# Two row groups for B.C, and a new order of the work around it, in a two-directional state-space kernel

## The chip, the cores and the metric

The kernel runs on one core of one Trainium2 chip. A core has five engines that run side by side and meet at semaphores: TensorE (PE in the profile; its weight loads, which overlap its matmuls, are PEld), VectorE (DVE), ScalarE (ACT), GpSimd (POOL) and SyncE (SP), which issues most of the DMAs. Matmuls write to PSUM[...]; everything else lies in SBUF. The metric is the time of one execution in device microseconds.

## The reference

The input x is 8 sequences of 512 tokens with 256 features. Each goes through a layer norm, a state-space layer in both directions and a linear layer with a low-rank correction:

```python
def _mamba2(x, Win, convw, convb, dtb, Alog, Dsk, normw, Wout):
    z, xBC, dt = split(x @ Win)                  # 512, 512 + 64 + 64, 8
    xBC = _silu(causal_conv4(xBC, convw) + convb)
    xs, Bm, Cm = split(xBC)                      # xs: 8 heads of 64
    dt = softplus(dt + dtb)
    dA = exp(dt * -exp(Alog))
    h_t = dA_t * h_{t-1} + outer(dt_t * xs_t, B_t)
    y_t = C_t . h_t + Dsk * xs_t
    y = y * _silu(z)
    y = y * rsqrt(mean(y * y) + 1e-05) * normw
    return y @ Wout

x = x + concat([fwd(ln(x)), flip(bwd(flip(ln(x))))]) @ Wo + bo
x = x + (ln(x) @ W.T + b + (ln(x) @ V_r) @ C.T)
```

Everything is computed in float32.

## The kernel before

A sequence is cut into four chunks of 128 tokens (NC = 4). Inside a chunk the recurrence becomes matrix work: B.C of all pairs of tokens of the chunk (a 128x128 matrix per direction, `cb`), times the decays between the two tokens, which a scan on VectorE makes (`scan`), gives the matrix `lam` (`mix` multiplies the two); `lam` times the scaled inputs `xdt` gives the chunk's own part of y, and the state at the chunk's edge times `dec` (decays times C) gives the rest. A **pair** is chunk c of the forward direction with chunk 3 - c of the backward one; there are 32, and the main loop (line 817) takes one per pass, i = 0 to 31. Pass i finishes pair p = i (`outputs`, `evict`, `times_gate`, `square`) and prepares pair q = i + 1 (`turn`, `cb`, `gate`, `scale_x`, `scan`, `skip`, `mix`, `scale_c`). Between them stand up to four blocks of a later sequence's projection and convolution (`work[0]` to `work[3]`: `project` on TensorE, `tap` on ScalarE, `convolve` on VectorE, `silu` on ScalarE) and the tail of an earlier chunk (`t`: output projection `project`, `residual`; `t0`, one pass later: `scales`, `norm2`, `bias2`, `turn`, `ffn`, `add_ffn`). Every eight passes (two sequences) a group of short VectorE steps for softplus and the decays is added (`st`).

The order of the instructions on each engine is that of the program text: `pin` ties each instruction to the one before it on its engine. So moving a call moves it in every queue that it issues to.

**PSUM.** The banks are given out by four pools: `p_seed` 1, `p_proj` 3 (`pp` of a projection, `pz` of the gate, `pst` of the state), `p_tr` 2 (`pxs`, `pxt`, `pxh` and other transposes, `ss`, `ptot`, `pcb`) and `p_y` 2 (`py` of both directions, then `pf` and `pm` of the tail; `pwy` and `pwf` in the first passes). A tile waits for the bank's last reader.

**cb before.** For one pair, B of both directions stands in 128 partitions (`bb`: 64 state rows of the forward direction, then 64 of the backward one). C stands twice: in `cc`, laid out like `bb`, for `scale_c`, and in `cbd`, block-diagonal, 128 columns per direction with zeros elsewhere. One matmul of 128 rows and 256 columns gives both directions' B.C. `silu` of the block that holds B and C writes all three copies (line 421), each of 64 partitions x 512. Memsets at line 171 zero `cbd`.

Names that the change and the steps touch, with their lines: `Block.silu` L415/L423, `Pair.turn` L496/L498, `scale_x` L507, `cb` L514, `mix` L520, `skip` L528, `gate` L538, `gate_silu` L545, `decay_state` L553, `outputs` L563, `add_state` L583 to L589, `evict` L593, `times_gate` L597, `square` L600, `norm_sum` L605, `norm_mean` L609, `norm_power` L612, `presum` L618; `Tail.bias1` L633, `project` L640, `residual` L647, `norm2` L657, `bias2` L668, `turn` L673/L675, `ffn` L680, `add_ffn` L683; `prepare_wf` L212/L213; `scale_c` L479; `steps_last` L345, `steps_total` L361; `turn1` L257/L258; `tokenwise_b` L432/L434.

Of the kernel before, what the change touches and what calls it, by code (L numbers as in the profile page):

```python
# [8 lines left out]
F32 = mybir.dt.float32  # L9
AF = mybir.ActivationFunctionType  # L10
ALU = mybir.AluOpType
# [3 lines left out]
P = 128  # L15
NB, L, DM = 8, 512, 256
NC = L // P
DI = 512
NS = 64
# [12 lines left out]
def tile_bimamba_ffn(  # L32
# [55 lines left out]
    def ps(p, shape, name):  # L88
        return p.tile(shape, F32, name=name, tag=p.name)
# [76 lines left out]
    pool.tensor_tensor(fold, ident[:, :64], ident[:, 64:], ALU.add)  # L166

    cbd = []
    for i in range(2):
        cbd.append(const.tile([P, NC, 2, P], F32, name=f"cbd{i}"))  # L170
        pool.memset(cbd[i], 0.0)

# [193 lines left out]
    class Block:  # L366
# [45 lines left out]
        def silu(self):  # L412
# [7 lines left out]
            bs, cs = slice(0, NS), slice(NS, P)  # L420
            for to, rows in ((s["bb"], bs), (cbd[b % 2][:, :, d, :], cs), (s["cc"], cs)):
                half = to[d * NS:(d + 1) * NS]
                act.activation(  # L423
                    half if d == 0 else half[:, ::-1, :],
                    self.acc[rows, :].rearrange("p (c t) -> p c t", c=NC), AF.Silu,
                )
# [12 lines left out]
    class Pair:  # L439
# [71 lines left out]
        def cb(m):  # L511

            m.pcb = ps(p_tr, [P, 2, P], f"cb_{m.name}")
            pe.matmul(  # L514
                m.pcb.rearrange("p d t -> p (d t)"), lhsT=m.s["bb"][:, m.c, :],
                rhs=cbd[m.b % 2][:, m.c].rearrange("p d t -> p (d t)"), start=True, stop=True,
            )

        def mix(m, d):
            dve.tensor_tensor(  # L520
                m.lam[d], m.lam[d], m.pcb[:, d, :].unsqueeze(1).to_broadcast([P, NH, P]), ALU.mult
            )
# [54 lines left out]
        def add_state(m):  # L577
            if m.c == NC - 1:
                return
            pst = ps(p_proj, [P, DI], f"pst_{m.name}")  # L580
            for d in range(2):
                rows = slice(d * NS, (d + 1) * NS)
                pe.matmul(pst[rows, :], lhsT=m.s["bn"][:, m.c, rows], rhs=m.xw[d], start=True, stop=True)  # L583
            if m.c == 0:
                m.h_new = m.tile("h", (P, DI))
                act.copy(m.h_new, pst)
            else:
                dve.tensor_tensor(m.h_new, m.h_new, pst, ALU.add)
            m.s["h"] = m.h_new  # L589
# [227 lines left out]
    for i in range(n):  # L817
# [12 lines left out]
        if (c == 0 if even else c == 1) and b + 3 < NB:  # L830
            load(b + 3)
        when(t0, "scales", "norm2", "bias2")
        p.decay_state()
# [4 lines left out]
        p.add_state()  # L838
        when(before, "norm_sum", "norm_mean")
        if q:  # L840
            for d in range(2):
                q.turn(d)
        when(work[0], "project", "tap")
        when(t0, "turn")
# [5 lines left out]
        if st and not even and c == 2:  # L850
            st.exponential()
        if q:
            q.cb()
            q.gate(0)
            q.gate_silu(0)
            for d in range(2):
                q.scale_x(d)
            q.scan(0)
        if q:
# [8 lines left out]
        if st and not even and c == 2:  # L868
# [3 lines left out]
            pairs[i + 2].fetch()  # L872
        when(t0, "ffn", "add_ffn")
        when(before, "norm_power")
        if q:
            q.scale_c()
        when(t, "bias1")
        p.presum()
# [15 lines left out]
        if i < 2:  # L894
            prepare_wy(i, range(2, NBLK))
        if q:
            q.skip(1)
        when(work[1], "convolve")
        if i == 2:
            prepare_wf()  # L900
        if i == 0:
# [10 lines left out]
        if even and c in (1, 3) and ahead < NB:  # L912
            turn1(ahead + (c == 3), 0)
            turn1(ahead + (c == 3), 1)
        if c == 2 and b + 1 < NB:
            tokenwise_b(b + 1)
# [75 lines left out]
```

## Time and profile before

| What | Value |
|---|---|
| median of 3 runs | 665.66 us (665.1 to 667.6) |
| the profiled execution | 668.52 us, its span 666.5 us |
| granted TensorE clock, mean of the span | 0.983 |
| matmul records of cb (L514) | 64, mean 397 ns, 20.1 us in all |
| SiLU into cbd (L423) | 16, median 628 ns |
| scale_c (L479) / bias1 (L633) / bias2 (L668), one | 2.36 / 0.73 / 0.73 us |
| GpSimd's bias2 waits for ScalarE's norm2 | 71.5 us in all, 29 times |
| VectorE's convolution waits for ScalarE's tap | 41.9 us in all, 24 times |
| VectorE's residual waits for GpSimd's bias1 | 16.5 us in all, 10 times |

How to read it: the profile is one execution with a hardware profiler. A row of a timeline has the start, the length, the engine, the line of the kernel, the operation, output<-inputs, the shape, and xN for N records that follow each other; in brackets stands how long the engine had been idle before, and what ended that. A float32 matmul leaves two records (four for a sum over two halves of the features); [...]the rate is read from start to start. A wait for several semaphores is put down to the last one by the profile. A row of the table of stretches has start:end and length, then for each engine its busy time and number of instructions, in the order PE, PEld, DVE, ACT, POOL, then the granted clock, the DMA share and GB/s.

### The profile page before, as it was taken

Reading aid. Unit: us, or ns where it says so; the run is one execution under the profiler, and the core shown is the slowest. Engines: PE = TensorE matmul, PEld = TensorE weight load, DVE = VectorE, ACT = ScalarE, POOL = GpSimd, SP = SyncE. Lnnn points to the kernel's source line nnn. Section 1 sums busy time; section 2 is a strip of 40 time slices with the busy share of each in tenths; the row PEclk is TensorE's granted clock in tenths of the full one; section 3 lists DMA queues with packets and bytes.
Section 4 is the critical chain, followed back from the end, with each engine's and each line's share of the span. In section 5 each row is a group of like instructions: output and inputs, shape, how many; then the busy total and the mean of one; then the engine's idle time right before and its main releaser. Section 6 shows DMA issues by size and latency. Waiting matters only on the chain.

```text
span 666.5 us, 12446 instructions
## 1 busy us (share of the span) xinstructions
PE 623.3 (94%) x4652; PEld 478.5 (72%) x4652; DVE 542.0 (81%) x827; ACT 399.8 (60%) x855; POOL 467.2 (70%) x572
## 2 busy tenths in 40 slices
PE   4968998999999999999999999999999998999996
PEld 2556676777776777877777677777877777787785
DVE  4788888788988899977988998877998887886643
ACT  2787565876566565875476574686576654564421
POOL 4447455677854888757856789638876679599983
PEclk9979998999999999999999998999999998999998
DMA  7555332313055312134045322332005432333010
GB/s 207 161 168 143 111 104 49 86 42 102 18 182 142 112 62 90 59 92 143 17 135 147 92 64 80 112 112 103 25 13 179 104 111 80 111 112 111 17 49 32
DMA packets 34940, 64.63 MB, mean 97 GB/s; under 512 B 7680, under 2 KB 22080, under 8 KB 34880
## 3 DMA queue, kind: packets, MB, share of 16 engines
q1 hardware_dynamic: 32736, 63.79, 31.8%
q8 instruction: 37, 0.61, 0.4%
q10 hardware_dynamic: 2144, 0.04, 0.2%
q14 instruction: 23, 0.19, 0.1%
HBM read 59.10 MB, written 4.72 MB: 96 GB/s over the span
## 4 chain that ended last, share of the span: by engine, by line
PE 51%; DVE 24%; POOL 13%; ACT 7%; issue 4%; DVEq 0%; POOLq 0%; ACTq 0%
PE pm L640 11%; PE pp L379 9%; PE pz L538 9%; PE py L563 9%; DVE xc L397 7%; DVE lam L490 4%; PE pf L680 3%; POOL yg L597 3%; DVE lam L520 3%; PE pxs L496 3%; POOL xdt L507 2%; PE pdt L275 2%; DVE x L647 2%; ACT xc L390 2%; PE pst L583 2%
## 5 line engine op out<-in xcount | busy, mean ns | idle before, releaser
L397 DVE SCALAR_TENSOR_TENSOR xc<-pp,conv_sb,xc 128x511 f32<-128x511 f32 x183 | 136.0, 744 | 46.3 <-ACT xc L390 41.9
L379 PE MATMUL pp<-xhT,win_sb 128*128 128x512 f32 x320 | 151.2, 600 | 0.5 <-ACT xhT L710 0.5
L490 DVE TENSOR_TENSOR_SCAN lam<-lam,seed 128x512 f32<-128x512 f32 x128 | 145.6, 1200 | 0.0
L538 PEld LDWEIGHTS pz<-xhT,win_sb 128*128 128x128 f32 x1024 | 125.7, 194 | 10.3 <-issue 7.7
L538 PE MATMUL pz<-xhT,win_sb 128*128 128x128 f32 x1024 | 126.6, 277 | 0.0
L640 PE MATMUL pm<-wy,yg 128*128 128x256 f32 x512 | 115.5, 379 | 0.0
L640 PEld LDWEIGHTS pm<-wy,yg 128*128 128x128 f32 x512 | 97.1, 190 | 13.1
L379 PEld LDWEIGHTS pp<-xhT,win_sb 128*128 128x128 f32 x320 | 57.8, 194 | 45.7 <-issue 42.6
L528 ACT ACTIVATE yg<-xc,dcol 128x128 f32<-128x128 f32 x256 | 80.9, 393 | 0.0
L390 ACT ACTIVATE xc<-pp,conv_sb 128x512 f32<-128x512 f32 x64 | 49.3, 774 | 44.9 <-PE pp L379 44.7
L520 DVE TENSOR_TENSOR lam<-lam,cb 128x1024 f32<-128x1024 f32 x64 | 75.0, 1212 | 0.1
L668 POOL TENSOR_TENSOR x<-x,bf_sb 128x256 f32<-128x256 f32 x32 | 23.3, 729 | 73.6 <-ACT xh L657 71.5
L507 POOL TENSOR_TENSOR xdt<-xs,dw 128x512 f32<-128x512 f32 x64 | 66.5, 1046 | 6.6 <-ACT xs L498 6.6
L563 PE MATMUL py<-lam,xdt 128*64 128x128 f32 x1024 | 66.3, 285 | 0.0
L415 ACT ACTIVATE xc<-xc 128x512 f32<-128x512 f32 x64 | 39.5, 628 | 43.7 <-DVE xc L397 43.4
L563 PEld LDWEIGHTS py<-lam,xdt 128*64 128x64 f32 x1024 | 58.6, 143 | 7.5 <-issue 4.6
L593 DVE TENSOR_TENSOR yg<-py,yg 128x512 f32<-128x512 f32 x64 | 42.2, 685 | 18.0 <-PE py L563 15.5
L507 POOL TENSOR_TENSOR xs<-xs,dw 128x512 f32<-128x512 f32 x48 | 50.1, 1045 | 3.8
L647 DVE SCALAR_TENSOR_TENSOR x<-pm,rms,x 128x256 f32<-128x256 f32 x64 | 30.9, 483 | 25.4 <-POOL x L633 16.5
L496 PE MATMUL pxs<-ident,xc 128*128 128x128 f32 x256 | 39.7, 286 | 12.5 <-ACT rms L609 5.1
L498 ACT COPY xs<-pxs 128x512 f32<-128x512 f32 x64 | 36.1, 586 | 15.4 <-PE pxs L496 15.2
L496 PEld LDWEIGHTS pxs<-ident,xc 128*128 128x128 f32 x256 | 29.8, 151 | 19.2 <-ACT rms L609 6.8
(445 smaller groups left out, 996.0 us busy)
## 6 DMA issues: line engine op xcount, KB each, us to landing
lam<-dat SPq DMA_DIRECT2D x64, 512.0 KB, 5.2
x<-in_x_dram SPq DMA_DIRECT2D x36, 128.0 KB, 2.2
out_dram<-x SPq DMA_DIRECT2D x32, 128.0 KB, 1.7
x<-in_x_dram SPq DMA_DIRECT2D x7, 512.0 KB, 6.8
win_sb<-in_win_dram SPq DMA_DIRECT2D x2, 640.0 KB, 5.8
win_sb<-in_win_dram SPq DMA_DIRECT2D x2, 512.0 KB, 7.9
wot<-in_wout_t_dram SPq DMA_DIRECT2D x2, 512.0 KB, 12.4
wo_sb<-in_wo_dram SPq DMA_DIRECT2D x2, 256.0 KB, 8.9
```

The lines of the kernel that those rows point to most:

```text
L379: pe.matmul(pp, lhsT=win_sb[:, d, k, c0:c0 + P], rhs=s["xhT"][:, k, :], start=(k == 0), stop=(k == NK - 1),)
L390: act.activation(self.acc, self.pp, AF.Identity, bias=self.w[:, 4:5], scale=self.w[:, 3:4])
L397: dve.scalar_tensor_tensor(self.acc[:, to], self.pp[:, of], self.w[:, 3 - j:4 - j], self.acc[:, to], ALU.mult, ALU.add,)
L490: dve.tensor_tensor_scan(lam, lam, sd, 0.0, ALU.mult, ALU.add)
L496: pe.transpose(pt[:, blk * P:(blk + 1) * P], m.s["xc", d][:, blk, m.tcol[d]], ident)
L507: pool.tensor_tensor(hb(to), hb(m.xw[d]), dw[:, j, cols].unsqueeze(2).to_broadcast([P, NH, HD]), ALU.mult)
L520: dve.tensor_tensor(m.lam[d], m.lam[d], m.pcb[:, d, :].unsqueeze(1).to_broadcast([P, NH, P]), ALU.mult)
L528: act.activation(yg[:, blk, :], m.s["xc", d][:, blk, m.tcol[d]], AF.Copy, scale=dcol[:, d, blk:blk + 1])
L538: pe.matmul(pz[:, blk, :], lhsT=win_sb[:, d, k, blk * P:(blk + 1) * P], rhs=m.s["xhT"][:, k, m.tcol[d]], start=(k == 0), stop=(k == NK - 1),)
L563: pe.matmul(m.py[d][two * HD:(two + 1) * HD, blk, :], lhsT=lhsT, rhs=rhs, start=first, stop=last, skip_group_check=True,)
L640: pe.matmul(t.pm[:, d, :], lhsT=yg[:, blk, :], rhs=wy[:, d, blk, :], start=(blk == 0), stop=(blk == NBLK - 1),)
L647: dve.scalar_tensor_tensor(t.x1[:, 0, :], t.pm[:, d, :], t.s["rs", d, t.c], t.x1[:, 0, :], ALU.mult, ALU.add)
```

## The change

B.C of a pair becomes two matmuls, one per direction, each of 64 rows (its own half of `bb` and `cc`) and 128 columns, into two PSUM tiles of `p_tr`. `cbd`, its memsets and its SiLU go. In the loop:

- `cb` moves behind `gate(0)`;
- where the pass has a block `work[0]`, `norm2` of the tail moves behind the pair's `turn`, and `bias2` behind `scale_x`; in passes without one they stay;
- `add_state` keeps its matmuls, and its copy or addition becomes `new_state`, behind `norm_mean`;
- `bias1` moves in front of `norm_power` and `scale_c`;
- `prepare_wf` (pass 2) moves in front of `work[1]`'s convolution;
- `skip(1)` moves behind `gate(1)`, `gate_silu(1)` and `turn1`.

```diff
-    cbd = []
-    for i in range(2):
-        cbd.append(const.tile([P, NC, 2, P], F32, name=f"cbd{i}"))
-        pool.memset(cbd[i], 0.0)
...
-            for to, rows in ((s["bb"], bs), (cbd[b % 2][:, :, d, :], cs), (s["cc"], cs)):
+            for to, rows in ((s["bb"], bs), (s["cc"], cs)):
...
         def cb(m):
-            m.pcb = ps(p_tr, [P, 2, P], f"cb_{m.name}")
-            pe.matmul(
-                m.pcb.rearrange("p d t -> p (d t)"), lhsT=m.s["bb"][:, m.c, :],
-                rhs=cbd[m.b % 2][:, m.c].rearrange("p d t -> p (d t)"), start=True, stop=True,
-            )
+            m.pcb = [ps(p_tr, [P, P], f"cb_{m.name}_{d}") for d in range(2)]
+            for d in range(2):
+                rows = slice(d * NS, (d + 1) * NS)
+                pe.matmul(
+                    m.pcb[d], lhsT=m.s["bb"][rows, m.c, :], rhs=m.s["cc"][rows, m.c, :], start=True, stop=True
+                )
...
         def mix(m, d):
             dve.tensor_tensor(
-                m.lam[d], m.lam[d], m.pcb[:, d, :].unsqueeze(1).to_broadcast([P, NH, P]), ALU.mult
+                m.lam[d], m.lam[d], m.pcb[d].unsqueeze(1).to_broadcast([P, NH, P]), ALU.mult
             )
...
         def add_state(m):
             if m.c == NC - 1:
                 return
-            pst = ps(p_proj, [P, DI], f"pst_{m.name}")
+            pst = m.pst = ps(p_proj, [P, DI], f"pst_{m.name}")
             for d in range(2):
                 rows = slice(d * NS, (d + 1) * NS)
                 pe.matmul(pst[rows, :], lhsT=m.s["bn"][:, m.c, rows], rhs=m.xw[d], start=True, stop=True)
+
+        def new_state(m):
+            if m.c == NC - 1:
+                return
             if m.c == 0:
                 m.h_new = m.tile("h", (P, DI))
-                act.copy(m.h_new, pst)
+                act.copy(m.h_new, m.pst)
             else:
-                dve.tensor_tensor(m.h_new, m.h_new, pst, ALU.add)
+                dve.tensor_tensor(m.h_new, m.h_new, m.pst, ALU.add)
             m.s["h"] = m.h_new
...
-        when(t0, "scales", "norm2", "bias2")
+        when(t0, "scales")
+        if work[0] is None:
+            when(t0, "norm2", "bias2")
         p.decay_state()
         p.outputs()
         for d in range(2):
...
             p.times_gate(d)
         p.add_state()
         when(before, "norm_sum", "norm_mean")
+        p.new_state()
         if q:
             for d in range(2):
                 q.turn(d)
+        if work[0] is not None:
+            when(t0, "norm2")
         when(work[0], "project", "tap")
         when(t0, "turn")
...
         if q:
+            q.gate(0)
             q.cb()
-            q.gate(0)
             q.gate_silu(0)
             for d in range(2):
                 q.scale_x(d)
+        if work[0] is not None:
+            when(t0, "bias2")
+        if q:
             q.scan(0)
...
         when(t0, "ffn", "add_ffn")
+        when(t, "bias1")
         when(before, "norm_power")
         if q:
             q.scale_c()
-        when(t, "bias1")
         p.presum()
...
         if i < 2:
             prepare_wy(i, range(2, NBLK))
-        if q:
-            q.skip(1)
+        elif i == 2:
+            prepare_wf()
         when(work[1], "convolve")
-        if i == 2:
-            prepare_wf()
...
             turn1(ahead + (c == 3), 0)
             turn1(ahead + (c == 3), 1)
+        if q:
+            q.skip(1)
         if c == 2 and b + 1 < NB:
             tokenwise_b(b + 1)
         when(work[1], "silu")
```

## The prediction

> **What bounds the kernel now.** I read the page's first and fourth parts, then the table of stretches, then the waits of each engine inside those stretches. "Pair i" is pass i of the loop over 32 pairs, some 19 us each.
>
> ```profile
> PE 623.3 (94%) x4652; PEld 478.5 (72%) x4652; DVE 542.0 (81%) x827; ACT 399.8 (60%) x855; POOL 467.2 (70%) x572
> ...
> PE 51%; DVE 24%; POOL 13%; ACT 7%; issue 4%; DVEq 0%; POOLq 0%; ACTq 0%
> ```
>
> TensorE is busy 94%, but the chain that ends last is only half TensorE. The table of stretches says why.
>
> ```profile
> 250.00:322.00 72.00, 72.00 (x525) 56.21 (x522) 61.37 (x84) 48.10 (x103) 53.04 (x62) 1.00 0.29 89
> 322.00:401.00 79.00, 74.62 (x571) 56.59 (x569) 70.69 (x114) 50.76 (x109) 57.68 (x70) 1.00 0.32 97
> ```
>
> The two kinds alternate. From 250 to 322 us (as from 401 to 478) TensorE has no gap. From 322 to 401 (as at about 165-248 and 485-555) TensorE idles 4.4 us, and VectorE sets the pace: it has no pause above 0.12 from 308 to 346, and afterwards it stops only for others. Two of those stops, on VectorE:
>
> ```profile
> 366.70 2.32 DVE L397 SCALAR_TENSOR_TENSOR xc<-pp,conv_sb,xc 128x511 f32<-128x511 f32 x3 [2.72 <-ACT xc L390]
> ...
> 380.18 1.00 DVE L647 SCALAR_TENSOR_TENSOR x<-pm,rms,x 128x256 f32<-128x256 f32 x2 [0.70 <-POOL x L633]
> ```
>
> The first is a convolution waiting for its tap on ScalarE, which stands behind three SiLUs; the second is `residual` waiting for `bias1` on GpSimd, which stands behind `norm_power` and `scale_c`:
>
> ```profile
> 364.08 0.63 ACT L423 ACTIVATE bb<-acc 64x512 f32<-64x512 f32 x1 [1.91 <-DVE acc L397]
> 364.72 0.63 ACT L423 ACTIVATE cbd<-acc 64x512 f32<-64x512 f32 x1
> 365.25 0.61 ACT L423 ACTIVATE cc<-acc 64x512 f32<-64x512 f32 x1
> 365.89 0.78 ACT L390 ACTIVATE xc<-pp,conv_sb 128x512 f32<-128x512 f32 x1
> ```
>
> ```profile
> 377.10 2.36 POOL L479 TENSOR_TENSOR dec__3525<-dec__3525,cc 128x1024 f32<-128x1024 f32 x1
> 379.42 0.73 POOL L633 TENSOR_TENSOR x<-x,bo_sb 128x256 f32<-128x256 f32 x1
> ```
>
> **What the Trainium skill says.** "TensorEngine Tiling (Array Packing)", Key Properties: changing the tiling mode, not just the tile, drains TensorE. The trace agrees; the only full-width row-tiled matmuls (32 rows x 128 columns, `pwf`) show the price:
>
> ```profile
> 101.58 1.88 PE L379 MATMUL pp<-xhT,win_sb 128*128 128x512 f32 x4
> 103.39 1.12 PE L212 MATMUL pwf<-ct_sb,vt_sb 32*128 32x256 f32 x4
> 104.45 2.05 PE L538 MATMUL pz<-xhT,win_sb 128*128 128x128 f32 x16
> ```
>
> Four `pp` matmuls take 1.72 from start to start where the mode stays, here 1.81: 0.09 of drain. Four records of 256 columns take 0.86 (8 take 1.73 at L640), here 1.06: 0.20, the first weights unhidden and the drain out. The next `pz` run lasts 2.05 where 1.95 is usual: its weights, 0.10. One excursion costs 0.39. "TensorE: Matmul & The Clock Gate", Part 3: matmuls in different row groups run at once. The trace agrees: the 64x64 `dec` matmuls at L563 need 1.03 us for 32 (306.74 to 307.77), 32 ns each, where full-array ones of the same 128 columns (`pz`) need 110. The tiling page's Gotcha 1 says different row tiles must write different PSUM banks; no run here shows it, but the two `pcb` tiles fit it and so take both `p_tr` banks.
>
> **The change, part by part.**
>
> *cb.* Now two records of 256 columns, 0.44 us:
>
> ```profile
> 313.91 0.60 PE L514 MATMUL cb<-cbd,bb 128*128 128x256 f32 x2
> 314.35 1.95 PE L538 MATMUL pz<-xhT,win_sb 128*128 128x128 f32 x16
> ```
>
> After: two matmuls of two records of 128 columns (0.11 each). If the groups run side by side, two steps, 0.22. Its neighbours (`gate(0)` before; `pf` or `pm` after) use the full array, so 0.39 is added: 0.61, or +0.17 per pair. Bounds: no excursion price, 0.22 - 0.44 = -0.22; no overlap of the first and last record, 0.33 + 0.39 - 0.44 = +0.28. I take +0.18. It counts where TensorE has no wait: the chain holds cb 18 times; leaving out three inside VectorE's stretches and the prologue's leaves 14: +2.5 us. The other pairs absorb it.
>
> *Later cb, two banks.* Behind `gate(0)` (1.78 us) both older tiles of `p_tr` are copied out (xT at 370.94-371.30, cb then at about 372). The mix on VectorE comes 6 us after cb: no wait. `turn1`, `tokenwise_b` and `steps_total` now wait for both mixes; at 398.02 `turn1` would wait 0.4 us in front of a wait that is already there (1.1); behind it stand turn1's second half and the next `py`, which `residual` holds until 401.1 anyway. Nothing. In the last four work-free pairs cb waits 0.29 for pxs' copy today (581.15 against 580.86); the gate covers that: 0.29 in each of three such pairs, -0.9.
>
> *cbd's SiLU gone.* 16 of 0.63 us on ScalarE. The chain holds them at 36.46, 44.55, 70.67, 210.39, 364.72 and 519.63. At 44.55 `cc` takes its place as cb's operand: no gain. So 0.63 in the prologue, 0.63 in pair 0, and 0.63 in each of VectorE's three stretches. Its two memsets (3.1 to 4.9 us) are covered by ScalarE's DMA issues and table load, which end at 8.7: 0 to 0.4, taken as 0.
>
> *bias1 before norm_power and scale_c, bias2 behind scale_x.* From the end of scale_x, `residual` was free after 0.72+2.36+0.73 = 3.8; now after bias2, bias1, norm_power 2.2: 1.6 earlier, more than the VectorE waits on it (0.70 and 0.13 in each stretch). `scale_c` ends 1.46 later and `py` needs it: at pair 17 about 400.8 before shifts, against `py` at 401.1 today, so still in time. Each stretch then gains 0.63 + 0.70 + 0.12 = 1.45; three: 4.4.
>
> *norm2 behind the turn copies, new_state behind norm_mean, skip(1) later.* norm2 (0.60) leaves the head of ScalarE's pair, so `rms`, for which `pxs` waits 5.1 us in all, is earlier. Those waits lie in VectorE's stretches: nothing on the end. Behind norm2 then stand the first tap and xT's chain (`pxt`, `pf`): `pxt` follows the last pxs by 1.7 us of `pp`, and copy and norm2 take 0.6 + 0.6 of them. `add_ffn` needs bias2 at 379.1 and would have it at 377.2. skip(1) (1.27) goes behind `gate_silu(1)` and turn1's copies; cost only in pairs 3, 11 and 19, where the tap of the third block comes 0.6 later, covered by VectorE's 0.35 wait for `py` and TensorE's lead: 0. In pair 0 it frees `ptot` (TensorE waits 1.65), but VectorE leads there.
>
> *prepare_wf before the convolution (pair 2).*
>
> ```profile
> 108.24 2.29 DVE L397 SCALAR_TENSOR_TENSOR xc<-pp,conv_sb,xc 128x511 f32<-128x511 f32 x3
> 110.44 0.75 DVE L213 TENSOR_TENSOR wf<-pwf,wt_sb 128x256 f32<-128x256 f32 x2
> ```
>
> ```profile
> 110.95 1.97 PE L563 MATMUL py<-dec__866,h__873 64*64 64x128 f32 x32 [2.41 <-POOL ln_nm L232]
> ```
>
> `py` there waits 2.41 us; the page names ln_nm, done at 110.3, but the bank comes free with the first wf at 110.86. With wf first, `py` starts when TensorE is ready, about 107.7 (108.4, less 1.26 from the two SiLUs, plus three cb). But VectorE's later convolution ends only 0.4 sooner (1.07 gained, 0.75 lost to wf), and the next `pxs` needs it: it starts at about 114.0 and `pp` at 114.4 instead of 117.23. Today half-clock (0.50 from 111.6 to 115.0) makes up 1.7 of that and may come again. Between 1.1 and 2.8 I take 2.0, the SiLUs' 1.26 included.
>
> *The end.* In pairs 28 to 30 GpSimd has no pause:
>
> ```profile
> 603.39 1.00 DVE L647 SCALAR_TENSOR_TENSOR x<-pm,rms,x 128x256 f32<-128x256 f32 x2 [3.91 <-POOL x L633]
> ```
>
> ```profile
> 604.45 1.09 PE L563 MATMUL py<-dec__5723,h__5767 64*64 64x128 f32 x28 [0.78 <-DVE x L647]
> ```
>
> Then `residual` is early and `py` waits for scale_c instead: 1.78 after today's scale_c becomes 0.73, 1.05 saved, once, since GpSimd's sum per pair (603.4 to 619.8: 16.4) is unchanged. No DMA moves in any step; SP's queue stays as it is.
>
> **Sum** against the profiled execution, 668.52 us (span 666.5): +2.5 - 0.9 - 4.4 - 2.0 - 1.1 = -5.9, so 662.6. That run lies 2.9 above the median of 665.66, so I carry the difference over: 659.8, or 0.9% less.
>
> **Rivals.**
> 1. Slower: the excursion of cb. Price +0.28 in all 31 loop pairs, 8.7 us, if row groups don't overlap and TensorE is tight everywhere, with only half of the 8.4 gained: 665.7 + 8.7 - 4.2 = 670.2. For it: the 0.39 is measured. Against: 4.4 us of TensorE idle time in each VectorE stretch. With all gains, it decides from 8.4/31 = 0.27 per pair.
> 2. No change: VectorE's freed time is not passed on, because TensorE, with its own cb, has no room in the stretches: 665.7 + 2.5 - 0.9 - 2.0 - 1.1 = 664.2. For it: TensorE is continuous in pairs 24 and 25. Against: it then still waits 1.2 + 0.6 us for `py`'s banks.
> 3. The row tiles cost no excursion: -0.22 x 14 = -3.1 in place of +2.5: 654.2. `pwf` speaks against it.
>
> **How the numbers follow.** Forecast 0.52, rival 1 0.15, rival 2 0.20, rival 3 0.13. A measurement tells about 0.5% (3.3 us) from no change. Faster: 0.46 of the forecast's cases, rival 3, a little of rival 2: 0.64. Slower: 0.15. The rest 0.21. Three half-clock windows of 3.4 us, 1.7 each, may come or go with any shift. Range 654.5 to 667.5: cb's bounds (-3.1 to +4), half the gains, one window more.
>
> **What would show it.** cb: four records, 0.6 from its start to the next run's, with about 0.1 of gap before. The waits of xc on ACT at 366.7 down to 2.1; `residual` without waits on bias1; `py` of pair 3 without 2.4; `py` of pairs 29, 30 waiting for `dec`. Wrong if cb takes 0.25 or 0.8, if `py` starts to wait for `dec` in every stretch, or if `pbn`/`pxh` wait for the mixes.

## The result and the profile after

The changed kernel takes 659.56 us (median of 5 runs, 658.6 to 660.04) against 665.1 before (5 runs, 662.96 to 667.6): 0.9913 of it, 95% interval 0.9888 to 0.9937. The forecast was 659.8, 0.9% less. The profiled execution of the changed kernel took 659.56 us, its span is 657.7.

The page's first and fourth parts, of the changed kernel:

```profile
PE 621.0 (94%) x4716; PEld 473.5 (72%) x4716; DVE 542.0 (82%) x827; ACT 391.1 (59%) x839; POOL 464.0 (71%) x570
...
PE 48%; DVE 27%; POOL 11%; ACT 8%; issue 4%; DMA 2%; ACTq 0%; POOLq 0%; DVEq 0%
```

64 matmul records more and TensorE is still busy 94%; ScalarE is 8.7 us shorter (16 SiLUs of 0.63 are 10.1), GpSimd 3.2. The bound is the same pair of engines by turns. The table of stretches, for the same two kinds of stretch (from, to, length, then the busy time of PE, PEld, DVE, ACT and POOL, the clock and the DMA's share):

```profile
246.70:318.70 72.00, 72.00 (x529) 56.01 (x529) 61.35 (x84) 46.22 (x98) 51.92 (x61) 1.00 0.29 87
318.70:396.80 78.10, 75.21 (x599) 56.91 (x601) 71.05 (x116) 50.70 (x110) 57.61 (x71) 1.00 0.34 99
```

In the first TensorE has no gap, as before. In the second it idles 2.9 us where it idled 4.4, and the stretch is about a microsecond shorter.

Now the single places. First cb and its neighbours on TensorE:

```profile
310.20 0.38 PE L673 MATMUL pxt<-ident,xh 128*128 128x128 f32 x2
310.42 1.95 PE L534 MATMUL pz<-xhT,win_sb 128*128 128x128 f32 x16
312.30 0.49 PE L511 MATMUL cb<-cc,bb 64*128 64x128 f32 x4
312.72 1.13 PE L680 MATMUL pf<-wf,xT 128*128 128x256 f32 x4
```

A run of `pz` lasts 1.78 from start to start when nothing changes; here cb starts 1.88 after it, so 0.10 is drain. From cb to `pf` it is 0.42, and `pf` lasts 1.13 where it lasted 1.03 (0.10, its first weights in the open). 0.10 + 0.42 + 0.10 = 0.62, and 0.43 before: +0.19 per pair.

ScalarE in the third block of a VectorE stretch, and VectorE waiting for its last line:

```profile
360.68 0.63 ACT L418 ACTIVATE bb<-acc 64x512 f32<-64x512 f32 x1 [0.91 <-DVE acc L392]
361.32 0.63 ACT L418 ACTIVATE cc<-acc 64x512 f32<-64x512 f32 x1
361.98 0.78 ACT L385 ACTIVATE xc<-pp,conv_sb 128x512 f32<-128x512 f32 x1
```

```profile
362.78 2.32 DVE L392 SCALAR_TENSOR_TENSOR xc<-pp,conv_sb,xc 128x511 f32<-128x511 f32 x3 [2.20 <-ACT xc L385]
...
375.47 0.99 DVE L647 SCALAR_TENSOR_TENSOR x<-pm,rms,x 128x256 f32<-128x256 f32 x2
```

Two SiLUs instead of three, and the wait falls from 2.72 to 2.20. `residual` (the last line) has no wait in front of it, since `bias1` is now done early on GpSimd:

```profile
373.24 0.73 POOL L633 TENSOR_TENSOR x<-x,bo_sb 128x256 f32<-128x256 f32 x1
373.93 0.72 POOL L612 TENSOR_TENSOR rms<-rms,neghalf 128x2 f32<-128x2 f32 x1
374.62 2.36 POOL L474 TENSOR_TENSOR dec__3543<-dec__3543,cc 128x1024 f32<-128x1024 f32 x1
```

And `scale_c`, behind it, is now what `py` waits for at the ends of the three stretches (0.51, 0.51 and 0.47 at pairs 10, 18 and 26) and in pairs 29 and 30. Five lines of TensorE, of pair 3 (its `py` no longer waits, but the next `pxs` does), of pair 10, and of pairs 29 and 30:

```profile
108.11 1.11 PE L559 MATMUL py<-dec__864,h__871 64*64 64x128 f32 x32
...
114.10 0.33 PE L491 MATMUL pxs<-ident,xc 128*128 128x128 f32 x1 [1.55 <-DVE xc L392]
...
242.62 1.20 PE L559 MATMUL py<-dec__2173,h__2189 64*64 64x128 f32 x32 [0.51 <-POOL dec__2173 L474]
...
595.23 1.20 PE L559 MATMUL py<-dec__5761,h__5810 64*64 64x128 f32 x32 [0.78 <-POOL dec__5761 L474]
...
611.62 1.20 PE L559 MATMUL py<-dec__5904,h__5923 64*64 64x128 f32 x32 [1.79 <-POOL dec__5904 L474]
```

Where the time went is read best from the start of `py` in each pair, after minus before, from the two traces:

| part of the run | difference at its end | change within it | of that, half-clock windows |
|---|---|---|---|
| start to `py` of pair 4 | -2.78 | -2.78 | 0 (as many in both) |
| pairs 4 to 6 (TensorE leads) | -2.41 | +0.37 | 0 |
| pairs 6 to 11 (with VectorE's stretch) | -3.86 | -1.45 | 0 |
| pairs 11 to 14 (TensorE) | -3.31 | +0.55 | 0 |
| pairs 14 to 19 (VectorE) | -6.34 | -3.03 | -1.7 |
| pairs 19 to 22 (TensorE) | -5.78 | +0.56 | 0 |
| pairs 22 to 27 (VectorE) | -8.69 | -2.91 | -1.7 |
| pair 27 to the end | -8.79 | -0.10 | |

The last column needs a word. In these traces TensorE's granted clock drops to 0.50 for 3.4 us at a time, or for several such windows in a row. I estimate the cost of one at half its length, 1.7 us; in before, the two pairs with the windows at 401.7 and 555.3 us took 1.6 and 1.9 us longer than pair 10, which has the same work and no window. The profiled run of before has these two more than that of after, so the two spans differ by 8.8 us, of which about 3.4 lies in the windows; what is left, 5.4, agrees with the medians (5.5). Whether the change itself makes the windows fewer is not shown. Because of them the experiments below are compared at nearly equal mean clock as well as by their ratio. Over many runs the time of one kernel follows its mean clock (the kernel of experiment e11: 661.5 us at 0.992 in 14 runs, 663.5 at 0.986 and 0.987 in 5, 665.0 at 0.983 in 3): about 0.4 us for each 0.001.

### The profile page after: what moved, and what is told of

Read it like the earlier page. It is cut to its first block, busy times and chain, and to the rows that moved or that the text cites. A ratio compares the mean times of both kernels' runs of the same rounds, so it can differ in the third digit from the quotient of the medians.

```text
span 657.7 us, 12589 instructions
## 1 busy us (share of the span) xinstructions
PE 621.0 (94%) x4716; PEld 473.5 (72%) x4716; DVE 542.0 (82%) x827; ACT 391.1 (59%) x839; POOL 464.0 (71%) x570
## 4 chain that ended last, share of the span: by engine, by line
PE 48%; DVE 27%; POOL 11%; ACT 8%; issue 4%; DMA 2%; ACTq 0%; POOLq 0%; DVEq 0%
PE pp L374 11%; PE pm L640 9%; PE pz L534 9%; DVE xc L392 8%; DVE lam L485 6%; PE py L559 5%; PE pf L680 3%; DVE lam L516 3%; PE pxs L491 2%; PE pdt L270 2%; POOL xdt L502 2%; ACT xc L385 2%; POOL yg L597 2%; DVE yg L593 1%; ACT xc L410 1%
## 5 line engine op out<-in xcount | busy, mean ns | idle before, releaser
L534 PEld LDWEIGHTS pz<-xhT,win_sb 128*128 128x128 f32 x1024 | 123.4, 194 | 10.8 <-issue 8.6
L640 PEld LDWEIGHTS pm<-wy,yg 128*128 128x128 f32 x512 | 97.1, 190 | 13.2
L559 PE MATMUL py<-lam,xdt 128*64 128x128 f32 x1024 | 63.0, 276 | 0.0
L559 PEld LDWEIGHTS py<-lam,xdt 128*64 128x64 f32 x1024 | 55.2, 137 | 7.1 <-issue 4.3
L680 PE MATMUL pf<-wf,xT 128*128 128x256 f32 x128 | 36.6, 411 | 2.6 <-DVE x L683 1.4
```

Of the source, the lines that this page charges most:

```text
L534: pe.matmul(pz[:, blk, :], lhsT=win_sb[:, d, k, blk * P:(blk + 1) * P], rhs=m.s["xhT"][:, k, m.tcol[d]], start=(k == 0), stop=(k == NK - 1),)
L559: pe.matmul(m.py[d][two * HD:(two + 1) * HD, blk, :], lhsT=lhsT, rhs=rhs, start=first, stop=last, skip_group_check=True,)
L640: pe.matmul(t.pm[:, d, :], lhsT=yg[:, blk, :], rhs=wy[:, d, blk, :], start=(blk == 0), stop=(blk == NBLK - 1),)
L680: pe.matmul(t.pf, lhsT=t.xT[:, k, :], rhs=wf[:, k, :], start=(k == 0), stop=(k == NK - 1))
```

## The experiments

All are timed in rounds of 5 against the kernel before. The last column is the mean time of the runs with a granted clock of 0.985 to 0.989, and their number. The first four ran on one chip, the second four on another, the last four on a third; the kernel before took 665.5 us at such a clock on the first (22 runs), 666.3 on the second (7) and 666.0 on the third (21). The changed kernel's five runs are those of the section above; it was not timed again beside the experiments. So "more" or "less than the changed kernel at equal clock" compares runs of different sessions. With the width of the clock band, the few runs in most rows and the 0.8 us between chips, a difference of about 1 us in that column settles nothing by itself; the starts of `py` in the traces are the finer measure. A trace is one run, though, and the half-clock windows have to be taken out of it.

| kernel | median us | ratio to before, 95% interval | at equal clock, us |
|---|---|---|---|
| changed kernel | 659.56 | 0.9913 [0.9888, 0.9937] | 659.4 (5) |
| e1: cb in front of the gate | 674.56 | 1.0145 [1.0109, 1.0180] | 673.9 (2) |
| e2: block-diagonal cb, new order | 660.26 | 0.9931 [0.9911, 0.9951] | 661.8 (3) |
| e3: third SiLU kept | 663.10 | 0.9967 [0.9954, 0.9980] | 663.8 (13) |
| e4: block-diagonal by DMA | 658.57 | 0.9915 [0.9882, 0.9948] | 658.6 (2) |
| e5: bias1 back | 674.06 | 1.0107 [1.0078, 1.0135] | 672.1 (2) |
| e6: prepare_wf back | 659.74 | 0.9886 [0.9859, 0.9913] | 659.7 (1) |
| e7: skip(1) back | 657.41 | 0.9858 [0.9832, 0.9883] | 658.5 (2) |
| e8: norm2, bias2, new_state back | 659.14 | 0.9881 [0.9857, 0.9904] | 659.1 (2) |
| e9: e4, e7 and e8 together | 657.15 | 0.9879 [0.9851, 0.9907] | 657.2 (2) |
| e10: e9, and biases on VectorE at the end | 654.91 | 0.9847 [0.9816, 0.9878] | 655.5 (3) |
| e11: e5 and e8 together | 662.26 | 0.9948 [0.9933, 0.9963] | 663.5 (5) |
| e12: row groups alone, old order | 661.20 | 0.9943 [0.9928, 0.9958] | 662.3 (6) |

My theory was the prediction's: the row groups cost 0.19 us per pair on TensorE and save ScalarE its SiLU, the gain comes from two waits of VectorE (on the tap, on `bias1`), and cb had to go behind the gate to have its banks. The rivals: the row groups themselves are the gain; the order is indifferent.

**e1, the place of cb.**

```diff
         if q:
-            q.gate(0)
             q.cb()
+            q.gate(0)
             q.gate_silu(0)
```

> The changed kernel with cb back in front of the first gate. My theory: in this place the two row-group matmuls, each with a bank of its own, must wait until xT has been copied out of its bank, and that wait is bare: in the changed kernel's trace pxt ends at 310.42 and the copy of xT at 311.44, so cb would wait 1.0 us in each of the 14 pairs in which TensorE has no pause: 10 to 15 us more than the changed kernel, 670 to 675. The rival, that the place of cb is indifferent and the gate is no cover for anything: no change, 659.6.

14.5 us more than the changed kernel at equal clock. TensorE at the same pair, then the line of its table of waits:

```profile
315.01 0.49 PE L511 MATMUL cb<-cc,bb 64*128 64x128 f32 x2
316.00 0.49 PE L511 MATMUL cb<-cc,bb 64*128 64x128 f32 x2 [0.50 <-ACT xT L675]
316.41 2.05 PE L534 MATMUL pz<-xhT,win_sb 128*128 128x128 f32 x16
```

```profile
PE cb L511 <- ACT xT L675: 11.4, 23, 0.5
```

The first matmul gets the bank of the last `pxs`, the second stands in front of `xT`'s copy, and the two groups no longer run side by side. In a pair that TensorE leads the start of `py` falls back by 0.97 against the changed kernel (12 to 13, 13 to 14, 20 to 21); 0.50 of it is this wait in the open, the rest the two matmuls taken apart. So the gate in front of cb is no ornament: without it the row groups cost more than everything that the change gains. Where VectorE leads (7 to 8, 15 to 16, 23 to 24) nothing is lost.

**e2, the new order without the row groups.**

```diff
+        cbd.append(const.tile([P, NC, 2, P], F32, name=f"cbd{i}"))
+        pool.memset(cbd[i], 0.0)
...
-            for to, rows in ((s["bb"], bs), (s["cc"], cs)):
+            for to, rows in ((s["bb"], bs), (cbd[b % 2][:, :, d, :], cs), (s["cc"], cs)):
...
-            for d in range(2):
-                rows = slice(d * NS, (d + 1) * NS)
-                pe.matmul(
-                    m.pcb[d], lhsT=m.s["bb"][rows, m.c, :], rhs=m.s["cc"][rows, m.c, :], start=True, stop=True
-                )
+            pe.matmul(
+                pcb.rearrange("p d t -> p (d t)"), lhsT=m.s["bb"][:, m.c, :],
+                rhs=cbd[m.b % 2][:, m.c].rearrange("p d t -> p (d t)"), start=True, stop=True,
+            )
```

> The changed kernel in all its order, but with the block-diagonal operand restored: its memsets, the third SiLU of each direction, and one matmul of 256 columns behind the first gate. My theory: cb gives back 0.19 us in each of 14 pairs (-2.7), the third SiLU costs 0.52 us on VectorE's path in three stretches and about as much in pair 0 and the prologue (+2.6), the memsets 0.4: within 1.5 us of the changed kernel, 659 to 661; the gain of the change lies in its order. The rival, that the row groups are what gains: 664 to 666, as before.

660.26, 0.9931 of before: most of the gain stands without the row groups. It is 0.7 above the changed kernel by the median and 1.1 by the trace at pair 31 (as many half-clock windows up to there in both), inside the 1.5 that I allowed; at equal clock, over 3 runs, it is 2.4. Its pairs under TensorE's lead are 0.15 to 0.19 us shorter than the changed kernel's, those with three SiLUs longer.

**e12, the row groups without the new order.** The other half: the kernel before, with cb in row groups behind the gate, no block-diagonal operand, no third SiLU, no memsets; bias1, norm2, bias2, new_state, skip(1) and prepare_wf as before.

> The other half of e2: the kernel before with the row groups alone, that is, cb in two row groups behind the first gate, no block-diagonal operand, no third SiLU, no memsets; every reordering of the other engines undone. Theory: +0.19 us in each of 14 pairs (+2.7), third SiLU gone (-2.6), memsets gone (-0.5), the wait of cb for pxs covered by the gate (-0.9): -1.3, 0.2% less than before, ratio 0.995 to 1.000. The rival, that the two banks of p_tr make turn1 and tokenwise_b wait for the mixes: ratio above 1.002.

0.9943, just outside of my range of 0.995 to 1.000, though the interval reaches into it: the row groups alone gain more than I gave them. At pair 31 of the traces, with 1.7 us taken out for each half-clock window, they are 3.1 us ahead of before, the order alone (e2) 4.8 and both together 5.9. At equal clock it is 3.7, 3.7 and 6.1 to 6.9. So the larger part lies in the order by the traces, and the halves do not quite add up. Two terms of my sum were off. The price of cb was too high: 2.7, where e4 (below) finds 1.8. The third SiLU was perhaps too low (e3, next: 2.6 to 3.4). With these the sum gives -2.2 to -3.0, but it still counts the 0.9 of cb's wait, and in the last pairs, where that wait is, e12 gains only 0.2 (27 to 31). So the 3.1 is not fully accounted for. Neither half is the whole change: the rival "the row groups are what gains" falls by e2, and that all of it lies in the order by e12.

**e3, the third SiLU alone.** Kept as in e2, but written to a tile that nothing reads; cb stays in row groups.

> The changed kernel with only the third SiLU of each direction kept, written to a tile that nothing reads (the result is the same). My theory: ScalarE is on the path with it at two places in the start and in three of VectorE's stretches, where the traces of before and after differ by 0.52 us at the tap behind the SiLUs: 2 to 3 us more, 661.5 to 662.6. The rival, that ScalarE's 59% leave room and the SiLU was hidden: no change, 659.6.

+4.4 at equal clock, +3.5 by the median, +3.4 in the difference of the traces' `py` starts. I had expected 2 to 3: the direction is right, and the rival falls. ScalarE and VectorE at the place shown above:

```profile
363.07 0.63 ACT L419 ACTIVATE bb<-acc 64x512 f32<-64x512 f32 x1 [0.91 <-DVE acc L393]
363.71 0.63 ACT L419 ACTIVATE cbd<-acc 64x512 f32<-64x512 f32 x1
364.25 0.61 ACT L419 ACTIVATE cc<-acc 64x512 f32<-64x512 f32 x1
```

```profile
365.70 2.32 DVE L393 SCALAR_TENSOR_TENSOR xc<-pp,conv_sb,xc 128x511 f32<-128x511 f32 x3 [2.72 <-ACT xc L386]
```

The wait is 2.72 again, as in the kernel before: 0.52 for a SiLU of 0.63, because neighbouring activations overlap by 0.1. Each VectorE stretch takes about 0.5 of it; the start takes 2.1 up to `py` of pair 1. Not all of these 2.1 are the SiLU's: in this run the half clock of the start lasts until 53.8 us, two windows longer than in the changed kernel (48.5). e2 has the same SiLUs, and the memsets besides, without the longer half clock; it is 1.2 behind at that place. So the traces put the third SiLU at 2.6 to 3.4 us; that it costs more than the 3 of my expectation is not shown.

**e4, neither SiLU nor row groups.** The block-diagonal operand is filled from cc by two DMAs per sequence, a pass after the SiLUs; its zeros are written once.

```diff
+    def diagonal(b):
+        for d in range(2):
+            rows = slice(d * NS, (d + 1) * NS)
+            sp.dma_start(out=cbd[b % 2][rows, :, d, :], in_=seq[b]["cc"][rows])
...
+        if (c == 0 if b else c == 1) and b + 1 < NB:
+            diagonal(b + 1)
```

> The changed kernel with the block-diagonal operand filled by two DMAs from cc per sequence, a pass after the SiLUs, and its zeros written once by GpSimd in the prologue; cb of pair 0 stays in two row groups, all others are one full-array matmul of 256 columns. It has neither the third SiLU nor the change of mode. My theory: -0.19 us in each of 14 pairs where TensorE has no pause, 2.7 us less than the changed kernel: 656.5 to 657.5. Rival: the price of the row groups is not on the path (TensorE waits for VectorE over a whole round of pairs): 659.6. Second rival: the DMAs hold up the fetches behind them in SP's queue: above 660.

```profile
309.70 1.95 PE L548 MATMUL pz<-xhT,win_sb 128*128 128x128 f32 x16
311.49 0.60 PE L517 MATMUL cb<-cbd,bb 128*128 128x256 f32 x2
311.92 1.03 PE L694 MATMUL pf<-wf,xT 128*128 128x256 f32 x4
```

From `pz` to cb 1.79, from cb to `pf` 0.43, `pf` back at 1.03: no mode change, no drain. Against the changed kernel's trace each pair under TensorE's lead is 0.18 to 0.19 shorter, 1.8 at pair 31. That measures the price of the row groups, with its sign turned: 0.19 in a pair, but 1.8 over the run and not the 2.7 of 14 pairs, since VectorE's stretches give part of it back (0.35 from pair 9 to 10, 0.33 from 17 to 18). The times say less: 658.57 is a microsecond under the changed kernel, and the intervals overlap. A copy of 128 KB took 4.1 us from issue to landing (median); it has a pass of time, no engine waits for it in this trace, and the second rival, above 660, falls by the median.

**e5, bias1 back.**

```diff
-        when(t, "bias1")
         when(before, "norm_power")
         if q:
             q.scale_c()
+        when(t, "bias1")
```

> The changed kernel with bias1 again behind norm_power and scale_c. My theory: residual waits 0.70 us for it once more in each of the three stretches that VectorE leads, and in the last pairs bias1 comes 1.8 us later than it could; against that py's wait for dec at the stretches' ends (0.5 us each in the changed kernel) goes. Worked out: 3 x (0.70 - 0.5), to 3 x 0.82 if the waits for dec give nothing, plus 1.0 at the end: 1.6 to 3.5 us more than the changed kernel, 661.2 to 663.1. The rival, that one wait of GpSimd only took the other's place: 659.6.

12.7 us more at equal clock, not 1.6 to 3.5: by far the largest miss of an expectation. (The trace ends 13.2 later, of which two half-clock windows are about 3.4; so 10 to 13.) GpSimd, VectorE and TensorE at the end of the first stretch:

```profile
241.96 2.36 POOL L474 TENSOR_TENSOR dec__2173<-dec__2173,cc 128x1024 f32<-128x1024 f32 x1
244.27 0.73 POOL L633 TENSOR_TENSOR x<-x,bo_sb 128x256 f32<-128x256 f32 x1
```

```profile
245.04 1.00 DVE L647 SCALAR_TENSOR_TENSOR x<-pm,rms,x 128x256 f32<-128x256 f32 x2 [0.85 <-POOL x L633]
```

```profile
246.10 1.69 PE L559 MATMUL py<-dec__2173,h__2189 64*64 64x128 f32 x28 [1.17 <-DVE x L647]
```

`residual` waits for `bias1`, and `py` waits for the bank that `residual` holds; the wait goes through three engines, and here a half-clock window follows it (at 246.4; two more windows in this run than in the changed kernel's). But why 10 to 13, and not the 3.6 that the prediction gave to this order in the kernel before? In the changed kernel `bias2` stands behind scale_x instead of at the head of the pair, so 0.73 us more stands on GpSimd in front of `bias1`. That was my theory, which the next run tests.

**e11, to test that: bias1 back, and bias2, norm2 and new_state back at the head as well.**

> The changed kernel with bias1 behind norm_power and scale_c as in e5 (14 us slower than the changed kernel instead of 2), and norm2, bias2 and new_state at the head as in e8 (about 1 us faster). My theory after e5: bias2, put behind scale_x, pushes scale_c and bias1 0.72 us back, so with bias1 last residual waits over its pm banks and py behind it; with bias2 at the head, in GpSimd's wait for the evictions, the 0.72 is hidden and bias1's place costs what the prediction gave it: 1 to 3 us over the changed kernel, 660.5 to 662.5, a ratio of about 0.994. The rival, that bias1's place alone makes e5's loss: 670 and more.

662.26, 663.5 at equal clock, a ratio of 0.9948 where 0.994 was expected; the rival's 670 falls. So `bias1`'s place costs 4.4 us (e11 against e8; 3.8 in the traces, a window left out) with the three calls at the head, and 10 to 13 (e5 against the changed kernel) with them moved. The two edits belong together: e5, which has all of the change but the move of bias1, is slower than the kernel before. That it is `bias2`, and not norm2 or new_state, which goes with `bias1` is argued from their place on GpSimd; the three were not moved one by one. e11 differs from e12 only by the moves of skip(1) and prepare_wf: 0.9948 and 0.9943, and both are 2.8 behind the changed kernel at pair 31; so these two together are worth nothing that can be measured.

**e8, bias1 in front, and norm2, bias2 and new_state back at the head.**

```diff
-        when(t0, "scales")
-        if work[0] is None:
-            when(t0, "norm2", "bias2")
+        when(t0, "scales", "norm2", "bias2")
...
+        p.new_state()
         when(before, "norm_sum", "norm_mean")
-        p.new_state()
...
-        if work[0] is not None:
-            when(t0, "norm2")
...
-        if work[0] is not None:
-            when(t0, "bias2")
```

> The changed kernel with norm2 and bias2 again at the head of every pair and new_state in front of norm_sum and norm_mean. My theory, that of the prediction: nothing on the end, since where pxs waits for rms VectorE leads, 659.6 within 1 us. The rival: bias2 at the head (0.73 us) and norm2 in front of rms (0.6 us) delay the gate's products and pxs in all three VectorE stretches, 2 us or more, above 661.6.

0.3 below the changed kernel at equal clock; in the traces 1.0 ahead at pair 30, 0.36 to 0.38 in each VectorE stretch. The prediction's "nothing" stands within what was allowed, the rival falls. The gain lies where GpSimd's order shows: `bias2` is covered there by a wait that GpSimd has anyway,

```profile
245.88 0.72 POOL L668 TENSOR_TENSOR x<-x,bf_sb 128x256 f32<-128x256 f32 x1 [0.72 <-ACT xh L657]
```

and `py` at the end of the stretch no longer waits for dec, but 0.22 for its bank:

```profile
242.50 1.09 PE L559 MATMUL py<-dec__2173,h__2192 64*64 64x128 f32 x28 [0.22 <-DVE x L647]
```

The three moves were not taken apart, so which of them counts is open; the `dec` wait speaks for bias2.

**e6, prepare_wf back** behind the convolution of pair 2's second block.

> The changed kernel with prepare_wf again behind the convolution of pair 2's second block. My theory: py of pair 3 waits for the bank of the first pwf again, 2.2 us (in the difference of the traces py gains 2.3 us from pair 2 to pair 3), less what the later pxs waits for its xc now (1.55) and need not then: 0.7 to 2.3 us more, 660.3 to 661.9. The rival, that VectorE sets the pace there and the wait for the bank was cover: 659.6.

```profile
111.40 1.38 PE L559 MATMUL py<-dec__864,h__871 64*64 64x128 f32 x32 [1.88 <-POOL ln_nm L227]
```

`py` of pair 3 waits 1.88 again, the `pxs` behind it not at all, where it waits 1.55 in the changed kernel. Against the changed kernel `py` loses 1.95 at pair 3 and has 1.50 of it back at pair 4: the move is worth 0.45, under my lower end of 0.7. The rival, "the wait for the bank was cover", is nearly right. (This run's start was also 1.4 us later, before anything that the edit touches. In the eight kernels with this prologue, the changed one among them, `py` of pair 0 starts between 49.1 and 51.5; a microsecond there says nothing.)

**e7, skip(1) back** in front of that convolution.

> The changed kernel with skip(1) again in front of the convolution of the second block. The prediction had this move at nothing. The traces say more: in pair 0 ptot's wait of 1.65 us went, in pair 1 a wait of VectorE for a tap on ScalarE grew from 1.43 to 2.36 us, since skip(1) now stands behind turn1's copies. My theory now: py of pair 1 starts 1 to 1.7 us later than in the changed kernel, and pair 1 gives back 0.9, so the end lies 0 to 1 us later, 659.6 to 660.6. A rival, that pair 0's wait was TensorE's alone and VectorE leads from there: the move only costs, and the end lies 0.9 earlier, 658.7.

0.9 under the changed kernel at equal clock; in the traces +1.2 at pair 1, then -2.7 from pair 1 to 2, of which 1.7 is a half-clock window less. TensorE of e7, then TensorE and VectorE of the changed kernel:

```profile
76.08 0.66 PE L491 MATMUL pxs<-ident,xc 128*128 128x128 f32 x4 [1.32 <-ACT rms L609]
```

```profile
76.08 1.11 PE L491 MATMUL pxs<-ident,xc 128*128 128x128 f32 x4 [2.49 <-ACT rms L609]
```

```profile
93.32 2.32 DVE L392 SCALAR_TENSOR_TENSOR xc<-pp,conv_sb,xc 128x511 f32<-128x511 f32 x3 [2.36 <-ACT xc L385]
```

`pxs` starts at the same time in both: TensorE's 1.2 us gained in pair 0 stand one wait later as 1.2 more for `rms`, and that longer pause is followed by the window at 75.8 (the matmuls take 1.11, not 0.66). In pair 1 skip(1) stands behind turn1's copies and pushes a tap. Both halves of my expectation are there, and by the time the rival comes out. But at pair 3, the window left out, e7 is 0.3 behind; the rest of its lead, 1.0, comes in steps of 0.2 to 0.5 up to pair 29, which were not followed up.

**e9, the three together.**

> Three edits at once: the block-diagonal operand filled by DMA (e4), skip(1) back in front of the convolution (e7), norm2, bias2 and new_state back at the head (e8); bias1 stays in front of norm_power, prepare_wf in front of the convolution. If they are independent, their shifts in the traces, half-clock windows apart, add up: -1.8 (e4) -1.0 (e7: the 0.93 of pair 1 and what follows) -1.0 (e8) = -3.8 from 659.6, 655.8, a ratio to before of about 0.985. The rival, that two of them remove the same wait: 657 to 658.5, no better than e4 or e7 alone.

2.2 under the changed kernel at equal clock, not 3.8. e4's 1.8 and e8's 1.0 are in its trace; of e7 nothing is, for a half-clock window came back (at 114.6), and pair 0's 1.2 became 2.2. That 2.2 goes with two windows more at the start (half clock until 53.1 us, as in e3); e10, with the same prologue and without them, has 1.2 there. So e7's gain was mostly the window, and independent edits did not add up there.

**e10, e9 with bias1 and bias2 on VectorE in the last four pairs.**

```diff
-            pool.tensor_tensor(t.x1[:, 0, :], t.x1[:, 0, :], bo_sb, ALU.add)
+            (dve if late_pairs else pool).tensor_tensor(t.x1[:, 0, :], t.x1[:, 0, :], bo_sb, ALU.add)
...
+        late_pairs = i >= n - 4
...
         p.new_state()
+        if late_pairs:
+            when(t0, "bias2")
```

> As e9, and in the last four pairs and behind the loop bias1 and bias2 run on VectorE. Theory: in pairs 28 to 31 GpSimd is the bound (h waits for it twice, 2.07 us each, py for dec 0.78 and 1.79 in the changed kernel), VectorE has over 2 us of gaps per pair there; each pair takes two sums of 0.73 off GpSimd and puts two of 0.42 on VectorE: about 1.4 us in each of two or three pairs, 2 to 4 us less than e9. The rival, that TensorE or VectorE is next there at once: the same as e9.

654.91, 0.9847 of before and the fastest of all: 2.2 under e9, 1.7 at equal clock, at the lower end of my 2 to 4. `py` of pair 30 starts without a wait, 5.9 us sooner than in the changed kernel (e9: 1.8):

```profile
605.77 1.51 PE L573 MATMUL py<-dec__5868,h__5886 64*64 64x128 f32 x32
```

The trace of e10 is already 1.4 ahead of e9's at pair 28, where the edit begins (e9's slower start), 3.8 at pair 31 and 2.4 at the end, so in these two traces the edit gains 2.4 inside the loop and 1.0 in all (the last 8 us of e10 run at half clock, the last 6 of e9). So at the end GpSimd was the bound, as the prediction said, and taking load off it gained.

## Why the prediction was right, point by point

**The sum.** -5.9 was forecast, on the profiled time as on the median; the medians differ by 5.5, the traces without the windows by 5.4. The parts, beside the table of starts:

- *cb, +0.18 in a pair TensorE leads:* +0.37 + 0.55 + 0.56 = 1.48 in eight such pairs, 0.185 each; e4 takes it back. The price of one is right, with its working: drain, two steps of 0.1, weights in the open. The count is not: 14 pairs, 2.5 us, stand in the sum, since the chain holds cb so often, but 1.5 shows in the table and 1.8 in e4. Lying on the chain in a pair that VectorE also holds up does not make it a cost in full. Rival 1 (0.28, in all pairs) and rival 3 (no price) fall by the same rows. "Wrong if cb takes 0.25 or 0.8" did not happen; it takes 0.62.
- *VectorE's stretches, 1.45 each, -4.4:* -1.45, -1.33 and -1.21 without the windows, -4.0 in all, with the cb of the neighbouring pairs in them. Nearly right in sum; its terms were not. Rival 2, that TensorE has no room there, falls: it has 2.9 us of idle time left in the stretch shown. The traces of e8, e11 and e12 take a stretch apart: the row groups with two SiLUs gain about 0.6 to 0.75 (e12 against before, windows left out), `bias1`'s place 1.1 to 1.2 (e11 against e8) where the sum had 0.82, and the moves of norm2, bias2 and new_state lose 0.36 to 0.38 (e8), where the sum had nothing. On the lines themselves the SiLU takes 0.52 off the wait, not 0.63, and `py` waits 0.5 for dec at the end of each stretch. The step that `scale_c`, 1.46 later, is "still in time" was wrong by that much. It is one of the signs that I had named for being wrong ("if `py` starts to wait for `dec` in every stretch"), and it came; so did another, `pxh` waiting for the mixes (0.23 and 0.41 at 240.42 and 241.46 us). Neither was dear enough to stop the gain; e8, in which `py` there waits only 0.22 for its bank, suggests that the dec wait goes with the 0.36 to 0.38 that the moves lose.
- *bias1:* the waits of 0.70 are gone, and e11 against e8 puts 4.4 us on its place (3.8 in the traces), against 3 x 0.82 + 1.1 = 3.6 in the sum. The step counted bias1 and bias2 together ("1.6 earlier") and so did not see that bias2's move alone goes the other way.
- *norm2, bias2, new_state, nothing:* e8 says 0.3 to 1.0 lost by the move: small, but not nothing.
- *skip(1), "cost only in pairs 3, 11 and 19":* the step failed. I had not asked what stands behind skip(1) in pair 1, where turn1's copies come first: a tap there waits 0.93 longer (2.36 against 1.43). The note that in pair 0 it frees `ptot` "but VectorE leads there" was right: TensorE's gain was gone at the next `pxs`. The sum, 0, is what e11 and e12 show for it and prepare_wf together.
- *The start, -2.0:* -2.78 to pair 4, in two traces, of which the start alone scatters by a microsecond and more (see e6). Of this prepare_wf is 0.45 (e6), not the 0.7 that was left in the 2.0 beside the two SiLUs; the wait did move to `pxs` at 114.1, as said. For the SiLUs up to pair 1, where the sum had 1.26, e2 shows 1.2 with the memsets in it, and e3 2.1 with two more half-clock windows; the 1.26 stands. What else makes the 2.78 was not found.
- *The end, -1.1, and -0.9 for the wait of cb in the last pairs:* this is the largest miss, 2.0 forecast and 0.1 found: -0.6 from pair 27 to 31, and 0.5 lost behind it. The order of waits came as forecast (`py` waiting for dec, 0.78 and 1.79), but GpSimd's sum per pair is the bound there, and a wait changed its name more than its length.
- *Half-clock windows:* "may come or go with any shift". Two went in the profiled run. It was in the range, not in the sum.

The sum came within half a microsecond because its misses cancelled: cb cost 1.0 less than it stands for and the start gave 0.8 more, while the end gave 1.9 less and the stretches 0.4 less. That is luck. What is shown one by one is cb's price in a pair (e4), the need of its place (e1), that the SiLU was on the path (e3) and that bias1's place matters (e5, e11).

## What to carry to other kernels

Before a step on an in-order engine is moved, price it together with what else moves on that engine: `bias1` in front was worth 4 us with bias2, norm2 and new_state at the head and 10 to 13 with them moved, and no row of the profile before showed that. Where a matmul takes another mode of the array, count the drain, the weights left in the open on both sides, and the banks: here 0.19 us per pair behind the gate, 1.2 in front of it. Count them only in pairs where nothing else holds TensorE up; the chain's tally was too many. A wait that disappears has to be looked for at the next meeting of the same two engines, as `ptot`'s was at `pxs` and pair 3's `py` at the next `pxs`.

## What the runs showed of the hardware

- Each row-group matmul leaves two records, and in time the two first ones start together (at 0 and 6 or 7 ns, in 31 of the changed kernel's 32 pairs), the two second ones 213 to 214 ns later. That is the overlap of two row groups. The interval is twice the 107 of a 128-column step. In the pair shown above the weight loads of the second records start 107 ns after the first matmuls, and their matmuls another 106 ns later: I read this as weights in the open.
- A sum of 128x256 on VectorE with both inputs in SBUF took 0.41 us alone, and up to 1.70 beside GpSimd. Two lines of e10, VectorE's then GpSimd's:

```profile
588.67 1.70 DVE L647 TENSOR_TENSOR x<-x,bo_sb 128x256 f32<-128x256 f32 x1
```

```profile
587.73 2.36 POOL L480 TENSOR_TENSOR dec__5727<-dec__5727,cc 128x1024 f32<-128x1024 f32 x1
```

  It ends 0.28 after GpSimd's product does. The Trainium skill says as much ("SBUF — State Buffer", Who interferes with whom): the two engines share a pair of ports, and a VectorE sum with both inputs in SBUF waits while GpSimd reads there. I had priced the move at 0.42 each; e10 gained in spite of it.
- The half-clock windows inside the loop come at or just behind a pause of TensorE of 1.1 to 2.5 us in every trace here that has one, but the length of the pause does not decide it alone: a window comes with a wait of 2.49 us at 76.08 in the changed kernel and with one of 1.33 at 76.3 in e12, and none with the wait of 1.32 at 76.08 in e7. Why before had more of them, and whether the shorter waits are the reason, stays open.
